# Moving large loads, norm pieces, weight means and modulation copies in a three-layer transformer kernel

## The chip, the cores and the metric

The kernel runs on one core of one Trainium2 chip. The metric is device time in microseconds of one execution; the lower, the better. The core has five engines that each work through their own instruction stream in order: TensorE (PE, with its weight loads shown as PEld), VectorE (DVE), ScalarE (ACT), GpSimd (POOL) and SyncE (SP). A DMA is an instruction in the stream of the engine that issues it; the data are then moved by 16 DMA engines.

## The reference

x is [4, 512, 288] in float32: B = 4 batches of T = 512 tokens with C = 288 features, and a condition vector of 288 for each batch. The computation is a rotation of the features and three transformer layers:

```
x = rotate(x)                                       # x + (z R - z) U^T, z = x U, U from a QR of P, R = expm(skew(silu(c) W^T + b))
layer 1, 2:
  shift_a, scale_a, gate_a, shift_m, scale_m, gate_m = split(silu(c) @ W_ada + b_ada, 6)
  h = layernorm(x) * (1 + scale_a) + shift_a
  q, k, v = split(h @ W_qkv + b_qkv)                # 16 heads of 18; layer 2 normalises q and k per head, with gains
  x = x + gate_a * (softmax(q k^T / sqrt(18)) v @ W_proj + b_proj)
  h = layernorm(x) * (1 + scale_m) + shift_m
  x = x + gate_m * (gelu(h @ W1 + b1) @ W2 + b2)    # hidden size 1152
layer 3: the same attention; its MLP is a mixture of 4 experts, each token through its best 2
```

## The kernel before

**Stages.** The rotation comes first (some 150 us of the profile), then twelve attention blocks n = 0 to 11 (three layers of four batches, n = 4·layer + batch) in the function `attend`, with the MLP of the block before after each block of layers 1 and 2, and at the end the experts over 19 tiles of 256 tokens. The attention blocks lie between about 160 and 1,600 us.

**One block.** `attend` runs 32 steps. A step issues one `maxima` (two matmuls into PSUM tile p_s, and a reduction on VectorE) for a group of heads ten steps ahead, and one `weigh` (two matmuls into p_st, and an exponential on ScalarE into a tile e). p_s and p_st take turns in the two buffers of the PSUM tag "big"; so each p_st waits until the exponential of the step before has read its buffer, and each p_s until the last reduction has. Every second step takes two e tiles into `sum_values` (p_av), and every eighth copies the sum (o) with ScalarE and sends it out with DMAs (sd, od).

**Work beside the steps.** The rest of a step is taken from two lists of generators. `fill` yields pieces of TensorE work with a cost: the projections of the next block (p_qk, p_var, p_v), the output projection of the last block (p_o), the transposes of normalised rows (p_t), and in n=0 the modulations of layers 2 and 3 (`modulations`, p_mod and p_modT). `norms` yields pieces of VectorE work, one for each step: four statistics, the reciprocal square root, and four scaled rows xn for each `normalize`. What is left of both is issued when the 32 steps are over, and `layernorm` issues what is left of its own norm before it transposes.

**Means of the weights.** Layer 2 normalises its heads; for that `center_heads(1)` takes the mean of each head's 18 columns off the weights: three reductions on VectorE (two pieces of wqk, and brow), each followed by a multiplication and an addition on POOL. It is called before n=2.

**Loads.** `load` issues on SP's queue, pinned to the program's order. Weights are loaded by it during the steps: `load_mlp` (6 DMAs, 2.9 MB) at step 17 and `load_attn` (14 DMAs, 1.5 MB) at step 24 of n=1 and n=5; `fill_table` copies the experts' weights from their tensors into one table in device memory (etab), half an expert at step 20 of each of n=2 to 9. SP also issues the small transfers that carry q, k, v, o and the softmax sums through scratch tensors (qd, store, sd, od, oc, rd, rb). Each DMA carries one of eight completion semaphores, in rotation over the whole program; before it is issued, its engine waits for the last DMA that had the same one, unless that is known to have landed.

**Order.** Most instructions stand as a scheduler places them from the order in which the generators issue them; loads and everything in the rotation are pinned.

The loop that hands out pieces, in short:

```
for step in range(8 * NG):
    for begin in loads.get(step, ()):
        begin()
    maxima(ahead, mstep); E.append(weigh(G, s))
    if s % 2 == 0: give_values()
    next(norms, None)
    while left > 0: cost = next(fill, "end") ...
```

Of the kernel before, what the change touches and what calls it, by code (L numbers as in the profile page):

```python
# [16 lines left out]
B, T, C = 4, 512, 288  # L17
NT = 4
KC, KP = 3, 96
# [4 lines left out]
NG = 4  # L24
# [23 lines left out]
def cond_seq_kernel(ctx: ExitStack, tc: tile.TileContext, a: dict, out: bass.AP):  # L48
    nc = tc.nc
# [17 lines left out]
    dma = nc.sync.dma_start  # L67
# [11 lines left out]
    def pmm(name):  # L79
        return ps.tile([128, 512], F32, tag="mm", name=name, bufs=3)  # L80
# [7 lines left out]
    def row(v):  # L88
        return v.rearrange("(o n) -> o n", o=1)
# [49 lines left out]

    WA, WM = [], []  # L140

    def load(t, src):
        tc.keep_in_program_order(dma(t, src))

    def load_features(t, src):

# [35 lines left out]
    def center_heads(l):  # L182

        wqk, brow = WA[l][0], WA[l][3]
        parts = wqk[:, 0:KW, :], wqk[0:STRIPS * TAIL, KW:, :]
        for i, t in enumerate([w.rearrange("p k (h d) -> p (k h) d", d=HD) for w in parts]
                              + [brow.rearrange("p (h d) -> p h d", d=HD)]):
            m = wattn.tile([t.shape[0], t.shape[1], 1], F32, tag=f"wmean{i}", name=f"wmean{i}", bufs=1)
            vector.tensor_reduce(m, t, AX.X, ALU.add)
            nc.gpsimd.tensor_scalar_mul(m, m, -1.0 / HD)  # L190
            nc.gpsimd.tensor_add(t, t, m.to_broadcast(list(t.shape)))

    def projection_bias(l):

        wqk, wv, wp, brow, bv = WA[l]
        p = pmm(f"p_bv{l}")
        for m in range(NO):
            r = slice(0, QP if m < NO - 1 else LO)
            matmul(p[0:64, :C], bv[r, m, :], wp[r, m, :], start=(m == 0), stop=(m == NO - 1))
        vector.tensor_add(wp[0:64, NO - 1, :], wp[0:64, NO - 1, :], p[0:64, :C])  # L200
# [82 lines left out]
    def load_ada(n):  # L283

        w, bias = (("L1_cond_W_ada", "L1_cond_b_ada"), ("L2_cond_w_ada", "L2_cond_b_ada"),
                   ("L3_cond_w_adaln", "L3_cond_b_adaln"))[n // 2]
        wa = was[n] = borrow(n % 2, f"wa{n}", KP + 1, 3 * KC * C).rearrange("p (k n) -> p k n", k=KC)
        cols = slice(n % 2 * 3 * C, (n % 2 + 1) * 3 * C)
        load(wa[0:KP], a[w][:, cols].rearrange("(k p) n -> p k n", p=KP))
        load(wa[KP:KP + 1, KC - 1, :], row(a[bias][cols]))  # L290
# [6 lines left out]
    def modulations(ns):  # L297

        for n in ns:
            l, half = divmod(n, 2)  # L300
            if half == 0:
                mt = mts[l] = const.tile([128, 4, KW + 1, B], F32, name=f"modT{l}")
                nc.gpsimd.memset(mt, 0.0)
            gr = mods.tile([B, C], F32, tag="gr", name=f"gr{n}")
            p = pmm(f"p_mod{n}")
            for k in range(KC):
                for s in range(3):
                    matmul(p[s * 32:s * 32 + B, :C], scT[0:kk(k), k, :],
                           was[n][0:kk(k), k, s * C:(s + 1) * C], start=(k == 0), stop=(k == KC - 1))
                yield 0.5  # L310
            for s in range(2):
                q = (2 * half + s) * 32
                scalar.copy(md[q:q + B], p[s * 32:s * 32 + B, :C])
            scalar.copy(gr, p[64:64 + B, :C])
            dma(gtab[n * B:(n + 1) * B], gr)
            if half and l < 2:
                br = mods.tile([B, C], F32, tag="br", name=f"br{l}")
                load(br, row(a[("L1_cond_b_fc2", "L2_cond_b2")[l]]).to_broadcast([B, C]))
                nc.gpsimd.tensor_mul(br, br, gr)
                dma(btab[l], br)  # L320
            if n == 5:
                sr = mods.tile([B, C], F32, tag="br", name="sr")
                scalar.activation(sr, p[32:32 + B, :C], AF.Copy, bias=1.0)
                dma(mrow.rearrange("s b c -> (s b) c")[0:B], md[64:64 + B])
                dma(mrow.rearrange("s b c -> (s b) c")[B:2 * B], sr)
                dma(mrow.rearrange("s b c -> (s b) c")[2 * B:], gr)
            if n + 2 < 6:
                load_ada(n + 2)
            if half:
                if l:  # L330
                    yield "later"
                pt = pmm(f"p_modT{l}")
                for k in range(KW + 1):
                    w = 128 if k < KW else TAIL
                    transpose(pt[:w, k * 128:(k + 1) * 128], md[:, k * 128:k * 128 + w], ident)
                    for i in range(1 if k < KW else STRIPS):
                        scalar.copy(mts[l][i * TAIL:i * TAIL + w, :, k, :],
                                    pt[:w, k * 128:(k + 1) * 128].rearrange("p (s r) -> p s r", r=32)[:, :, :B])
                for s in (1, 3):
                    nc.gpsimd.tensor_scalar_add(mts[l][:, s], mts[l][:, s], 1.0)  # L340
                modT.append(mts[l])
                yield 0.6
# [20 lines left out]
    with tc.tile_pool(name="l0", bufs=1) as l0, tc.tile_pool(name="l0w", bufs=2) as l0w, \  # L363
# [199 lines left out]
        main, fills, side = skew_and_exp(), clear(), itertools.chain(project_P(), first_modulations())  # L563
# [466 lines left out]
    with tc.tile_pool(name="attn", bufs=2) as at:  # L1030
# [99 lines left out]

        def maxima(G, step):

            n, g = divmod(G, NG)
            j, hp = divmod(step, 2)
            p = pbig(f"p_s{G}_{step}")
            for i in range(2):
                r = slice((2 * hp + i) * HS, (2 * hp + i + 1) * HS)
                matmul(p[:, i, :], Q[n % 2][r, g, j * 128:(j + 1) * 128], K[n % 2][r, g, :], start=True, stop=True)
            vector.tensor_reduce(M[G % 2][:, j, 2 * hp:2 * hp + 2, HD:HD + 1], p, AX.X, ALU.max)

        def take_maxima(G):

            n, g = divmod(G, NG)
            p = pmm(f"p_m{G}")
# [74 lines left out]
        def attend(n, fill, total, norms, loads):  # L1219


            left, strips = 0.0, False
            for step in range(8 * NG):
                g, s = divmod(step, 8)
                G = NG * n + g
                for begin in loads.get(step, ()):
                    begin()
                ahead, mstep = divmod(8 * G + s + LOOK, 8)
                if ahead < NG * NB:
                    while ahead // NG not in there:  # L1230
                        next(fill)
                    maxima(ahead, mstep)
                E.append(weigh(G, s))
                filled = strips
                if strips:
                    left -= next(fill)
                    strips = False
                if s == 8 - 2 and G + 1 < NG * NB:
                    take_maxima(G + 1)
                    left -= 0.6  # L1240
                left += total / (8 * NG) + (0.5 if s % 2 else -0.5 if ready else 0.0)
                if s % 2 == 0:
                    give_values()
                next(norms, None)
                while left > 0:
                    cost = next(fill, "end")
                    if cost == "end":
                        break
                    if cost == "strips":
                        if filled:  # L1250
                            strips = True
                            break
                        continue
                    if cost == "later":
                        if filled:
                            break
                        continue
                    filled = True
                    left -= cost or 0.0
                if s % 2:  # L1260
                    ready.append((G, s // 2))
            for _ in fill:
                pass
            for _ in norms:
                pass
# [49 lines left out]
        E, ready, PO, S, there, norms = [], [], [None], {}, set(), {}  # L1315
# [34 lines left out]
        for n in range(NB):  # L1350
            l, b = divmod(n, B)
            last = n and divmod(n - 1, B)

            fill, side, total = [], [], 0.0
            loads = {}
            if n == 1 or n == B + 1:
# [2 lines left out]
                loads[24] = [lambda l=l, names=names: WA.append(load_attn(l + 1, *names))]  # L1359
                names = (("L1_cond_W_fc1", "L1_cond_b_fc1", "L1_cond_W_fc2"), ("L2_cond_w1", "L2_cond_b1", "L2_cond_w2"))[l]  # L1360
                loads[17] = [lambda l=l, names=names: WM.append(load_mlp(l, *names))]
            if n == 2 or n == B + 2:
                if l == 0:
                    center_heads(1)
            if n + 1 < NB:
                if n:
                    new = project(n + 1, norm)
# [11 lines left out]
            if n and last[0] < 2:  # L1379
                norm2 = normalize(last[0], 1, last[1], n - 1)  # L1380
                side.append(norm2)
                fill.append(layernorm(last[0], 1, last[1], hT[1], norm2))
                total += 1.8
            if n == NB - 3:
                prepare_routes()
                load_mods(0)
                load_mods(1)
# [204 lines left out]
```

## Time and profile before

| | us |
|---|---|
| median of 3 runs | 2043.26 |
| lowest and highest | 2023.45, 2050.5 |
| profiled execution | 2027.39 |
| its span, first to last instruction | 2025.7 |

The mean granted TensorE clock of the profiled execution was 0.963. ScalarE's largest group is the 384 exponentials, at 1023 ns each, VectorE's the 384 reductions, at 1226 ns:

```
L60 ACT ACTIVATE e<-p_st 128x1024 f32<-128x1024 f32 x384 | 392.7, 1023 | 643.2 <-PE p_st L60 639.7
L60 DVE TENSOR_REDUCE store<-p_s 128x2 f32<-128x1024 f32 x384 | 470.5, 1226 | 363.0 <-PE p_st L60 348.3
```

A row names the line, the engine, the operation, what is written from what, the shapes and the count; then the busy time and the mean of one in ns; then the idle time of the engine just before and what ended most of it. L60 is the line of a recording helper, through which most instructions pass, so groups are told apart by their tiles. In a waits view, a row gives the waiting engine and its tile, what it waited for, the total in us, the number of waits and the longest. In a timeline, the columns are start and length in us, engine, line, operation and tiles, the count, and in brackets the idle time before and what ended it. A "q" after an engine's name (SPq) is its queue, which issues DMAs and waits.

The work of `load` on SP in the profiled execution: `load_mlp` was issued at 349.25 and 878.80 us, `load_attn` at 66.72, 357.78 and 894.35 us.

### The profile page before, as it was taken

How to read it: one execution, taken by the hardware profiler on the slowest of the kernel's cores; microseconds unless marked ns; L12 is line 12 of the kernel's file. 1: busy time of each engine (PE TensorE's matmuls, PEld its weight loads, DVE VectorE, ACT ScalarE, POOL GpSimd, SP SyncE). 2: the span in 40 equal slices, each digit the busy share in tenths (PEclk: the TensorE clock that was granted, in tenths of full speed). 3: DMA queues.
4: the chain of work that ended last, by engine and by line, in shares of the span. 5: the costliest groups of instructions: out<-in, count | busy, mean ns of one | idle time of the engine just before them, and what ended most of it. 6: DMA issues, size and time to landing. Idle time of an engine off the chain costs nothing. (4 is left out here: it accounts for less than half of the span.)

```text
span 2025.7 us, 26353 instructions
## 1 busy us (share of the span) xinstructions
PE 1864.3 (92%) x10269; PEld 925.1 (46%) x10269; DVE 928.4 (46%) x1953; ACT 782.7 (39%) x1169; POOL 252.3 (12%) x362
## 2 busy tenths in 40 slices
PE   6769989999999999989999999999998899999997
PEld 4554222343523434435234343343332267788886
DVE  6764646446165263552652625535566534211111
ACT  5122355434354354443543444434444433122121
POOL 1000000010011010110110000010010132323232
PEclk9578999999999999999999999999999999999999
DMA  3311123312212123151110502144222265576673
GB/s 99 73 41 53 44 62 110 90 35 93 44 53 70 26 78 52 41 140 49 53 41 20 112 18 72 57 93 97 76 56 64 89 233 187 177 239 210 208 248 98
DMA packets 90283, 187.23 MB, mean 92 GB/s; under 512 B 26317, under 2 KB 51320, under 8 KB 87666
## 3 DMA queue, kind: packets, MB, share of 16 engines
q1 hardware_dynamic: 78326, 103.39, 19.3%
q0 software_dynamic: 11248, 79.79, 12.1%
q10 hardware_dynamic: 584, 2.36, 0.4%
q8 instruction: 81, 1.33, 0.3%
q14 instruction: 44, 0.36, 0.1%
HBM read 152.49 MB, written 55.45 MB: 103 GB/s over the span
## 5 line engine op out<-in xcount | busy, mean ns | idle before, releaser
L60 ACT ACTIVATE e<-p_st 128x1024 f32<-128x1024 f32 x384 | 392.7, 1023 | 643.2 <-PE p_st L60 639.7
L60 DVE TENSOR_REDUCE store<-p_s 128x2 f32<-128x1024 f32 x384 | 470.5, 1226 | 363.0 <-PE p_st L60 348.3
L60 PE MATMUL p_s<-store 32*128 32x512 f32 x1536 | 443.9, 651 | 75.4 <-DVE store L60 69.1
L60 PE MATMUL p_st<-store 32*128 32x512 f32 x1536 | 442.0, 651 | 1.3 <-DVE store L60 1.3
L60 PEld LDWEIGHTS p_s<-store 32*128 32x128 f32 x1536 | 117.9, 185 | 324.8 <-DVE store L60 253.2
L60 PE MATMUL p_av<-e,store 128*32 128x512 f32 x1536 | 211.2, 623 | 1.1 <-ACT e L60 1.1
L60 PE MATMUL p_he<-hTe,store 128*128 128x256 f32 (+1 forms) x1026 | 185.4, 387 | 1.4 <-DVE hTe L60 1.4
L60 PE MATMUL p_ye<-store,hide 128*128 128x288 f32 x684 | 171.1, 409 | 0.1
L697 POOL TENSOR_TENSOR x<-x,gated 128x288 f32<-128x288 f32 x80 | 63.9, 799 | 814.1 <-DVE gated L60 814.1
L60 PEld LDWEIGHTS p_he<-hTe,store 128*128 128x128 f32 (+1 forms) x1026 | 149.5, 189 | 33.7 <-issue 13.2
L60 PE MATMUL p_qk<-hT,wqk 128*126 128x512 f32 (+1 forms) x360 | 164.2, 621 | 0.3 <-DVE store L60 0.3
L60 ACT ACTIVATE hide<-p_he,store 128x256 f32<-128x256 f32 x171 | 68.2, 479 | 234.7 <-PE p_he L60 189.5
L60 PE MATMUL p_h<-hT,w 128*128 128x512 f32 (+1 forms) x432 | 153.5, 610 | 4.6 <-DVE store L60 4.6
L60 PEld LDWEIGHTS p_ye<-store,hide 128*128 128x128 f32 x684 | 128.4, 190 | 37.1 <-ACT hide L60 2.5
L60 DVE TENSOR_TENSOR gated<-p_y,gate 128x288 f32<-128x288 f32 x32 | 14.6, 458 | 282.6 <-PE p_y L60 282.6
L60 PE MATMUL p_y<-w,hid 128*128 128x288 f32 x576 | 141.8, 407 | 0.0
L60 PEld LDWEIGHTS p_y<-w,hid 128*128 128x128 f32 x576 | 108.8, 190 | 35.5 <-issue 6.1
L60 PEld LDWEIGHTS p_st<-store 32*128 32x128 f32 x1536 | 118.1, 186 | 9.0 <-issue 6.7
L60 PEld LDWEIGHTS p_h<-hT,w 128*128 128x128 f32 (+1 forms) x432 | 62.1, 189 | 91.2 <-issue 84.9
L60 PE MATMUL p_o<-wp,oc 126*128 126x288 f32 (+1 forms) x288 | 91.7, 438 | 0.8 <-DVE oc L60 0.8
L60 PEld LDWEIGHTS p_qk<-hT,wqk 128*126 128x126 f32 (+1 forms) x360 | 47.7, 178 | 95.2 <-issue 88.9
L1541 POOL DMA_INDIRECT out_dram<-ye,idx x38 | 60.9, 1603 | 209.9 <-issue 111.7
(248 smaller groups left out, 1672.4 us busy)
## 6 DMA issues: line engine op xcount, KB each, us to landing
store<-qd SPq DMA_DIRECT2D x192, 72.0 KB
qd<-stage SPq DMA_DIRECT2D x48, 252.0 KB
od<-o SPq DMA_DIRECT2D x192, 36.0 KB
rd<-rd SPq DMA_DIRECT2D x12, 576.0 KB
oc<-od SPq DMA_DIRECT2D x24, 252.0 KB
rb<-rd SPq DMA_DIRECT2D x24, 252.0 KB
etab<-in_L_cond_w_dram SPq DMA_DIRECT2D x4, 1296.0 KB
etab<-in_L_cond_w_dram SPq DMA_DIRECT2D x8, 576.0 KB
```

Source lines behind the costliest of these rows:

```text
L60: ins = f(*args, **kw)
L697: nc.gpsimd.tensor_add(x[b][:, j, :], x[b][:, j, :], t)
L1541: tc.keep_in_program_order(nc.gpsimd.indirect_dma_start(out_rows if t >= EARLY else out_rows[0:2 * T], bass.IndirectOffsetOnAxis(ap=idx[:, ...
```

## The change

Four edits. Loads that `attend` starts at a given step are issued on ScalarE's queue; other loads stay on SP's. From step 20 on, `norms` gives two pieces a step. `center_heads` becomes a generator with one of the three means as a piece, in the list of norms of n=2. And `modulations` yields after the copies that follow its last products and no longer between the products and the copies; the mark "later", with which `attend` put off p_modT of layers 2 and 3 until the next step, goes.

```diff
+    queue = [nc.sync]
+
     def load(t, src):
-        tc.keep_in_program_order(dma(t, src))
+        tc.keep_in_program_order(queue[0].dma_start(t, src))
...
     def center_heads(l):
...
             vector.tensor_reduce(m, t, AX.X, ALU.add)
             nc.gpsimd.tensor_scalar_mul(m, m, -1.0 / HD)
             nc.gpsimd.tensor_add(t, t, m.to_broadcast(list(t.shape)))
+            yield True
...
     def modulations(ns):
...
                 for s in range(3):
                     matmul(p[s * 32:s * 32 + B, :C], scT[0:kk(k), k, :],
                            was[n][0:kk(k), k, s * C:(s + 1) * C], start=(k == 0), stop=(k == KC - 1))
-                yield 0.5
+                if k < KC - 1:
+                    yield 0.5
             for s in range(2):
                 q = (2 * half + s) * 32
                 scalar.copy(md[q:q + B], p[s * 32:s * 32 + B, :C])
...
             if n + 2 < 6:
                 load_ada(n + 2)
+            yield 0.5
             if half:
-                if l:
-                    yield "later"
                 pt = pmm(f"p_modT{l}")
...
         def attend(n, fill, total, norms, loads):
...
             for step in range(8 * NG):
                 g, s = divmod(step, 8)
                 G = NG * n + g
+
+                queue[0] = nc.scalar
                 for begin in loads.get(step, ()):
                     begin()
+                queue[0] = nc.sync
...
-                    if cost == "later":
-                        if filled:
-                            break
-                        continue
                     filled = True
                     left -= cost or 0.0
+                if step >= 5 * NG:
+                    next(norms, None)
                 if s % 2:
                     ready.append((G, s // 2))
...
-            if n == 2 or n == B + 2:
-                if l == 0:
-                    center_heads(1)
...
+            if n == 2:
+                side.append(center_heads(1))
```

## The prediction

> **What bounds the kernel now.** I read four views, in this order: the page's first two parts, the waits of TensorE, the timelines around TensorE's longest gaps, and the queue views of SP and ScalarE. The page and the waits:
>
> ```profile
> span 2025.7 us, 26353 instructions
> PE 1864.3 (92%) x10269; PEld 925.1 (46%) x10269; DVE 928.4 (46%) x1953; ACT 782.7 (39%) x1169; POOL 252.3 (12%) x362
> PE p_s L60 <- DVE store L60: 69.1, 130, 2.2
> PE p_t L60 <- DVE xn L60: 6.3, 4, 1.6
> PE p_s L60 <- issue: 4.0, 1, 4.0
> PE p_modT L60 <- ACT md L60: 2.5, 2, 2.0
> ```
>
> TensorE is busy 92%, and in its 161 us of idle no DMA is named as releaser. What delays TensorE costs time nearly one to one; what delays SP costs nothing until a tile is missed. ScalarE's 39% looks roomy, but one step of `attend` is a tight ring: p_st goes out, ScalarE makes e from it, and the next p_st needs that PSUM buffer back, because the two `big` buffers alternate between p_s and p_st. In the timeline:
>
> ```profile
> 346.51 0.59 ACT L60 COPY o<-p_av 128x512 f32<-128x512 f32 x1
> 347.61 1.02 ACT L60 ACTIVATE e<-p_st 128x1024 f32<-128x1024 f32 x1 [0.51 <-PE p_st L60]
> 349.31 0.70 PE L60 MATMUL p_st<-store 32*128 32x512 f32 x2
> ```
>
> The exponential ends at 348.63 and the next p_st starts at 349.31: 0.68 us to spare. Elsewhere the spare is 2 to 3 us, counted from the start of ScalarE's instruction before it, since the queue can go on while that one runs.
>
> Gaps of TensorE, with what they do to the clock:
>
> ```profile
> 290.46 0.47 PE L60 MATMUL p_modT<-ident,md 128*128 128x128 f32 x1 [1.99 <-ACT md L60]
> 428.92 0.70 PE L60 MATMUL p_s<-store 32*128 32x512 f32 x2 [2.22 <-DVE store L60]
> 644.35 1.50 PE L60 MATMUL p_t<-ident,xn 128*128 128x128 f32 x4 [1.58 <-DVE xn L60]
> 893.53 1.19 PE L60 MATMUL p_s<-store 32*128 32x512 f32 x1 [4.05 <-issue]
> ...
> 644.00:648.00 4.00, 3.63 (x16) 1.87 (x16) 1.32 (x4) 1.55 (x2) 0.00 (x0) 0.64 0.00 0
> 894.00:898.00 4.00, 4.00 (x18) 0.95 (x14) 2.36 (x4) 1.02 (x1) 0.00 (x0) 0.54 0.78 209
> ```
>
> The last two are rows of the windows view (stretch, busy time of each engine, then granted clock, DMA share, GB/s). In the 4 us around the 1.58 us gap the clock was 0.64, about 3 us at half speed, with a little more in the next window: some 1.7 us lost besides the gap. After the 4.05 us gap it was 0.54 for 4 us: 1.8, and half a microsecond before it. After the 1.99 us gap the same sequence, from one p_s over p_m and p_av to the next p_s, took 4.69 us (292.56 to 297.25) where it took 2.65 at full speed (268.41 to 271.06): 2.0 lost.
>
> **The change part by part.**
>
> *Large loads.* The build moves 76 DMAs from SP to ScalarE, in twelve groups: 6 of `load_mlp` and 14 of `load_attn` in n=1 and n=5, and `fill_table`'s eight groups (6 or 3 DMAs) at step 20 of n=2 to 9. In ScalarE's order each group stands whole ahead of the next exponential, which queues behind it; behind that wait p_st, everything later on TensorE, and VectorE's reductions. Each issue takes its queue's time, and it first waits until the earlier DMA on its completion semaphore has landed (eight semaphores go round). On SP:
>
> ```profile
> 349.25 2.01 SPq L143 DMA_DIRECT2D w<-in_L_cond_W_fc_dram  x4
> 351.77 1.07 SPq L143 DMA_DIRECT2D w<-in_L_cond_W_fc_dram  x1
> 894.35 1.82 SPq L143 DMA_DIRECT2D wqk<-in_L_cond_w_qkv_dram  x4
> 901.18 0.23 SPq L143 DMA_DIRECT2D brow<-in_L_cond_b_qkv_dram  x1
> 903.15 0.25 SPq L143 DMA_DIRECT2D wp<-in_L_cond_b_proj_dram  x1
> 478.41 3.90 SPq L143 DMA_DIRECT2D etab<-in_L_cond_w_dram  x6
> 784.59 0.67 SPq L143 DMA_DIRECT2D etab<-in_L_cond_w_dram  x1
> 785.31 3.90 SPq L143 DMA_DIRECT2D etab<-in_L_cond_b_dram  x2
> ```
>
> brow waited until 901.18 for the first wqk piece, issued by 894.74: such a piece needs about 6.3 us to land. Now group by group, time of the block less ScalarE's spare:
> - `load_mlp`, n=1: the third DMA waits for the first, 1.2 MB, to land. A piece of half the size needed 6.3 us; a later DMA on this one's semaphore was issued at 357.02, so at most 7.3. I take 7.0: block from 346.5 to 356.5, exponential 8.9 late, less 0.7: 8.2.
> - `load_mlp`, n=5: it waits for the four od transfers of the o just copied, and then for a piece of its own weights; about 881.7 where the exponential stood at 874.3: 7.4 less 0.9: 6.5.
> - `load_attn`: 894.35 to 903.40 on SP is 9.05 (8.9 in the first one, from 66.72), less 3.1: 5.9, twice 11.8.
> - `fill_table` first half: 3.9 less 3.1 is 0.8 in n=2 and 8. In n=4 and 6 the last DMA comes round to a semaphore of its own group, so 1.2 of issue, 6.3 of landing and 0.6 make 8.1, less a spare of 2.1: 6.0 each. Together 13.6. Bounds for the latter two: 1.8 (landed at once) and 8 (a table-to-table copy twice as slow).
> - second half: 4.6 to 4.7, less 2.1 in n=3 and 5, less 3.1 in n=7 and 9: 8.4 together.
>
> Sum 48.5 (8.2 + 6.5 + 11.8 + 13.6 + 8.4). Clock: six stalls of 5 us and more at the 2.3 of the 4.05 us gap, and half of four stalls of 1.6 to 2.6 at 1.7: 17. Against it, VectorE catches up during a stall, and the p_s wait that would have come next (0.3 to 1.3 us) falls away: 12 times 0.7, 8. Net 57.5 lost.
>
> A rule is to be weighed here. The Trainium skill ("DMA: Bandwidth & Descriptors", Issuing engines are not separate DMA queues) says that starting DMAs on several engines saves only the sequencer's time for starting them, usually small beside the DMA itself. SP agrees that the saving is worthless: it waited 280.6 us for o copies alone. But "usually small" would put 76 issues at next to nothing on ScalarE too, and the sum would end at the gains below; the rows show 0.23 to 3.1 us an issue, and waits besides. I take the rows.
>
> What SP gains: its small transfers no longer stand behind large ones. No TensorE wait names them, so 0, except the 4.05 us gap at 893.53, in which TensorE waited for nothing shown while DMA was full; with its half clock 6.5. The same bytes move in the same steps, so it can as well recur: I take half, 3.2, bounds 0 and 6.5, or a second such gap, −6.5.
>
> *Two VectorE pieces in late steps.* `next(norms)` is called twice from step 20. By the build, the four xn of the MLP's norm, which in n=3 to 6 stood together behind the last reduction (1.44 us for four), now come one and two reductions earlier; the p_t gap of 1.58 falls away four times, with its clock: 4 x 3.3 = 13.1. Each late step carries up to 0.6 us more on VectorE; where the ring is tight p_s waits: 1 back. Gain 12, bounds 5 and 14. On the clock the skill's rule ("TensorE: Matmul & The Clock Gate", Part 1: The HAM clock gate) says that half rate follows an idle window of about 3.4 us; by it the 1.58 us gaps would cost no clock and this gain would be 6. The windows row of 0.64 decides for 12.
>
> *Means one by one.* Three reductions (2.00 us for two and 0.73, on VectorE in one go at 425.08, before n=2's first p_s reduction) go one to a step; POOL's part follows each, and POOL is idle 88%. The gap of 2.22 and its 1.7 go; the largest piece, 1.3 us, about fills VectorE's idle between two reductions (1.23 to 1.5 in the timeline), 0.3 back: gain 3.6. The weights are next read in n=3.
>
> *p_mod's copies.* They are issued in the step of the last products, and without "later" p_modT of layer 1 follows them directly, two steps sooner; layer 2's comes two exponentials after its copies. So layer 2's gap goes, 1.99 and 2.0 of clock, less 0.4 as its transposes now wait for an exponential as layer 1's did (1.00 against 0.56). But layer 1 gets the same gap: e, 1.02, and two md copies, 0.80, end about 1.6 us after p_mod does; 1.6 and 1.0 of clock (it cools in some such gaps), less 0.4. Gain 1.4, bounds −1 and 4. gtab and br leave SP and POOL earlier; nobody waits. In the rotation at the start the copies move by half a step under VectorE's chain: 0.
>
> Gains 3.2 + 12 + 3.6 + 1.4 = 20.2; 57.5 − 20.2 = +37. The profiled execution took 2027.4 us (its span 2025.7), so 2064 for one like it; it stood 16 below the median of the three runs, and on that median, 2043.3, it is 2080.
>
> **The rivals.**
> (1) ScalarE's blocks are short: not slower. Place: the twelve groups. If a load lands sooner on a queue of its own and the issues overlap the exponential before them, a block shrinks to its issue time, and the spare covers it. For: a spare of 2 to 3 us in ten of the twelve. Against: the third DMA of n=1 cannot be issued before 1.2 MB have landed. It decides where the stalls with their clock come under 20 us in all, 1.7 a group; with 3 left it is 2043 − 17 = 2026.
> (2) The round of semaphores ties the two queues together: ScalarE waits for SP transfers that are themselves held up, and SP's stores come due on the semaphores of ScalarE's w1 and w2. For: a store issue that took 3.63 us at 352.88, behind w2 on the same queue. Against: SP mostly waits for ScalarE, so it has caught up by then. Blocks 3 us longer in all twelve groups: 2080 + 36 = 2116.
> (3) The loads hinder nobody, before or after, and the gaps on VectorE's side come back elsewhere: 2043.
>
> **How the numbers follow.** Chances: forecast 0.57, its own range 2055 to 2105; (1) 0.2; (2) 0.19; (3) 0.04. A measurement of this kernel tells about 2% (41 us) from no change. Over 2% slower: 0.42 of the forecast, as 37 lies close under 41, and (2): 0.43. Over 2% faster needs every gain, no stall and 20 us more: 0.03. Within: 0.54. The range, 2026 to 2113, goes from (1)'s figure to just under (2)'s; half of each and little of the forecast are left out, 2 in 10.
>
> **What would show it.** DMA rows of `load` on ScalarE, 4 to 10 us a group; behind each an idle of TensorE before p_st or the next p_s, over 40 us in all, with clock windows of 0.5 to 0.7 after it; no p_t gap in n=3 to 6, and none over 1 us at n=2's first p_s; a p_modT gap that moves from layer 2 to layer 1. It is wrong if these stalls stay under 20 us in total, if ScalarE's groups last under 3 us, or if the p_t gaps stay.

## The result, and the profile after

| | before | changed |
|---|---|---|
| median, us | 2045.36 | 2105.94 |
| lowest and highest | 2023.45, 2050.50 | 2101.37, 2113.02 |
| runs | 4 | 4 |
| profiled execution, us | 2027.39 | 2103.59 |
| its mean granted TensorE clock | 0.963 | 0.936 |

The changed kernel is slower: the ratio is 1.032, with a 95% interval of 1.0239 to 1.0402. The forecast was 2080, in a range that went to 2113. The two profiled executions differ by more than the medians, by 76 us. Some 16 of it is a stretch of half clock in block 11, which the profiled execution of before happens not to have. By their times most runs of before have it too: they lie in two clusters, about 2027 and 2047 us, called the lower and the upper one below, and the last section tells of it. All four runs of the changed kernel have clocks of 0.935 to 0.938, like its profiled one, which has the stretch; three of the four of before are in the upper cluster. So the 60.6 us between the medians is like against like.

The first lines of the changed kernel's page, and rows of its view of TensorE's waits (tile, releaser, total in us, number, longest):

```profile
span 2101.9 us, 26331 instructions
PE 1924.6 (92%) x10269; PEld 945.3 (45%) x10269; DVE 929.4 (44%) x1953; ACT 783.0 (37%) x1169; POOL 252.5 (12%) x362
...
PE p_s L60 <- DVE store L60: 73.4, 138, 1.8
PE p_st L60 <- DVE store L60: 12.7, 8, 2.4
PE p_st L60 <- ACT e L60: 10.4, 5, 6.4
PE p_av L60 <- ACT e L60: 3.5, 2, 2.4
PE p_modT L60 <- ACT md L60: 1.4, 1, 1.4
```

The reader should see two things. First, new waits: p_st now waits for ScalarE's exponential (10.4 us) and for VectorE behind it (12.7, where it was 1.3 before), and p_av for e (3.5, where it was 1.1); the p_t wait is gone from the list and one of two p_modT waits is left. Second, these waits are far less than the time lost. TensorE's busy time rose by 60 us with the same 10,269 matmuls: more of them ran at half clock (the mean clock fell from 0.963 to 0.936).

How the one becomes the other is seen best at the smallest group of loads, `fill_table`'s in block 8. ScalarE's timeline, then TensorE's, then two rows of the windows view (the block from its first to its last exponential, and the 11 us after the group; the columns are the stretch, the busy time of PE, PEld, DVE, ACT and POOL, the granted clock, DMA share and GB/s):

```profile
1322.35 1.02 ACT L60 ACTIVATE e<-p_st 128x1024 f32<-128x1024 f32 x1 [1.37 <-PE p_st L60]
1322.36 3.74 ACTq L145 DMA_DIRECT2D etab<-in_L_cond_w_dram  x6
1326.20 1.02 ACT L60 ACTIVATE e<-p_st 128x1024 f32<-128x1024 f32 x1 [2.83 <-DMA etab<-in_L_cond_w_dram]
```

```profile
1322.19 1.92 PE L60 MATMUL p_o<-wp,oc 126*128 126x288 f32 x6
...
1328.94 1.75 PE L60 MATMUL p_st<-store 32*128 32x512 f32 x4 [1.33 <-DVE store L60]
1330.62 3.55 PE L60 MATMUL p_o<-wp,oc 126*128 126x288 f32 x6
```

```profile
1269.50:1360.60 91.10, 85.45 (x484) 29.00 (x483) 53.48 (x78) 42.30 (x52) 3.40 (x5) 0.94 0.23 71
1329.00:1340.00 11.00, 11.00 (x38) 3.87 (x38) 3.48 (x9) 2.44 (x4) 0.79 (x1) 0.53 0.08 26
```

Six issues hold ScalarE for 3.74 us. The exponential behind them comes 2.83 us late, and of that 1.33 reach TensorE. But the clock then falls to half for 10.2 us in which TensorE is busy all the time: the same six p_o matmuls take 3.55 us, where they took 1.92 just before. The block lasts 91.1 us, and 84.6 where the loads are on SP (below): here a stop of 1.33 us went with 6.5 lost. The last section shows the same stop without a fall of the clock.

The largest stop is in block 5, where `load_mlp`'s group waits for transfers to land. (Which one ends a wait is read from the trace's semaphore records: the second DMA was issued at 902.76, after a small copy of SP's had landed at 902.74, and the third at 906.87, after another at 906.85.)

```profile
899.06 1.01 ACT L60 ACTIVATE e<-p_st 128x1024 f32<-128x1024 f32 x1
899.90 0.40 ACTq L145 DMA_DIRECT2D w<-in_L_cond_w_dram  x1
899.96 0.58 ACT L60 COPY o<-p_av 128x512 f32<-128x512 f32 x1
902.76 4.91 ACTq L145 DMA_DIRECT2D w<-in_L_cond_w_dram  x3
907.72 0.44 ACTq L145 DMA_DIRECT2D b<-in_L_cond_b_dram  x1
908.19 1.46 ACTq L145 DMA_DIRECT2D w<-in_L_cond_w_dram  x1
909.70 1.02 ACT L60 ACTIVATE e<-p_st 128x1024 f32<-128x1024 f32 x1 [9.16 <-DMA w<-in_L_cond_w_dram]
```

```profile
910.78 2.08 PE L60 MATMUL p_st<-store 32*128 32x512 f32 x4 [6.41 <-ACT e L60]
```

From the first issue to the last ScalarE does nothing but one copy for 9.7 us; TensorE stands 6.41 us.

### The profile page after: what moved, and what is told of

It is laid out like the page before. It is cut to its first block, busy times and chain, and to the rows that moved or that the text cites. A ratio compares the mean times of both kernels' runs of the same rounds, so it can differ in the third digit from the quotient of the medians.

```text
span 2101.9 us, 26331 instructions
## 1 busy us (share of the span) xinstructions
PE 1924.6 (92%) x10269; PEld 945.3 (45%) x10269; DVE 929.4 (44%) x1953; ACT 783.0 (37%) x1169; POOL 252.5 (12%) x362
## 3 DMA queue, kind: packets, MB, share of 16 engines
q8 instruction: 81, 1.33, 0.3%
## 5 line engine op out<-in xcount | busy, mean ns | idle before, releaser
L60 PE MATMUL p_st<-store 32*128 32x512 f32 x1536 | 458.2, 673 | 23.1 <-DVE store L60 12.7
L60 PE MATMUL p_av<-e,store 128*32 128x512 f32 x1536 | 219.3, 645 | 3.5 <-ACT e L60 3.5
L60 PEld LDWEIGHTS p_y<-w,hid 128*128 128x128 f32 x576 | 108.8, 190 | 35.5 <-issue 6.1
L60 PE MATMUL p_o<-wp,oc 126*128 126x288 f32 (+1 forms) x288 | 109.3, 506 | 0.8 <-DVE oc L60 0.8
L60 PEld LDWEIGHTS p_h<-hT,w 128*128 128x128 f32 (+1 forms) x432 | 62.0, 189 | 91.2 <-issue 84.9
L60 PEld LDWEIGHTS p_av<-e,store 128*32 128x32 f32 x1536 | 31.0, 111 | 127.8 <-issue 121.1
```

The lines of the kernel that those rows point to most:

```text
L60: ins = f(*args, **kw)
```

## The experiments

The theory: the loads in groups on ScalarE cost the time, because a group stands whole ahead of the exponentials; the three other edits gain less than the prediction gave them. Rivals: a wait that the four edits make together; the second VectorE piece as the culprit; and a loss of each issue's time on ScalarE wherever it stands.

A table of block lengths carries most of what follows (us from the first to the last exponential of a block, from each profile's timeline; "start" is the first exponential of block 0):

| kernel | start | 0 | 1 | 2 | 3 | 4 | 5 | 6 | 7 | 8 | 9 | 10 | 11 |
|---|---|---|---|---|---|---|---|---|---|---|---|---|---|
| before | 215 | 83.4 | 84.9 | 87.4 | 92.7 | 92.7 | 99.7 | 92.7 | 83.8 | 83.9 | 84.9 | 96.5 | 86.4 |
| changed | 217 | 83.1 | 97.7 | 91.1 | 96.5 | 97.5 | 113.3 | 97.4 | 86.1 | 91.1 | 86.4 | 96.5 | 102.9 |
| loads on SP | 218 | 86.3 | 85.6 | 84.5 | 91.9 | 92.1 | 98.4 | 91.9 | 84.5 | 84.6 | 84.9 | 96.9 | 101.6 |
| loads alone | 215 | 83.5 | 97.6 | 91.3 | 98.6 | 98.3 | 116.3 | 99.7 | 85.5 | 91.1 | 86.5 | 98.0 | 101.6 |
| tables alone on ScalarE | 217 | 83.6 | 85.6 | 86.9 | 93.9 | 99.4 | 109.6 | 97.4 | 86.0 | 89.5 | 86.4 | 98.0 | 86.5 |
| one a step, ScalarE | 218 | 83.4 | 85.6 | 84.5 | 91.9 | 93.5 | 105.0 | 91.8 | 84.6 | 84.6 | 84.9 | 96.9 | 86.5 |
| groups on POOL | 216 | 82.0 | 85.6 | 84.7 | 103.2 | 92.6 | 108.5 | 91.9 | 84.5 | 84.6 | 84.9 | 98.5 | 99.9 |
| pieces early in a group | 219 | 83.4 | 84.8 | 83.8 | 91.0 | 91.0 | 98.4 | 91.0 | 83.8 | 83.9 | 84.9 | 96.5 | 103.2 |
| the same, p_mod as before | 215 | 83.4 | 84.9 | 83.8 | 91.0 | 90.9 | 98.2 | 90.9 | 83.8 | 83.9 | 84.9 | 96.5 | 86.4 |
| and one a step on SP | 216 | 82.7 | 84.9 | 84.0 | 91.0 | 90.9 | 90.9 | 90.9 | 83.8 | 83.9 | 84.9 | 100.3 | 86.4 |
| changed, no late pieces | 218 | 83.1 | 97.2 | 91.0 | 93.8 | 98.7 | 118.1 | 95.3 | 85.4 | 91.1 | 86.4 | 96.5 | 103.3 |
| loads on SP, dense matmul | 218 | 83.6 | 85.6 | 84.5 | 91.9 | 92.2 | 98.4 | 91.8 | 84.5 | 84.6 | 84.8 | 96.8 | 90.0 |
| one a step on SP, dense matmul | 215 | 82.7 | 84.9 | 84.0 | 91.0 | 90.9 | 90.9 | 91.0 | 83.8 | 83.9 | 84.8 | 100.3 | 102.6 |

What lies between the blocks differs by some 2 us at most; what follows block 11 takes 406 to 413 us. The medians of before that the ratios below refer to are 2044.89 us (13 runs) for the first four experiments, 2046.04 (31 runs) for the next four and 2046.80 (16 runs) for the last three. A median can lie in either cluster, so where a kernel's runs fall in both, the text also compares cluster with cluster.

**The changed kernel with its loads back on SP.**

```diff
-                queue[0] = nc.scalar
+                queue[0] = nc.sync
                 for begin in loads.get(step, ()):
                     begin()
```

> The changed kernel with its loads back on SP; the other three edits stay. Theory (ScalarE's stream is held up by the loads, everything else gains a little): below the kernel before by 10 to 25 us, about 2028, no wait of p_st for an exponential over 1 us, blocks n=3 to 6 each about 3 us shorter than before. Rival (the VectorE pieces or the modulation copies cost time too, for instance in n=11, which grew by 16 us): still above the kernel before, 2060 or more, with n=11 as long as in the changed kernel (103 us).

Measured: 2046.91 us, ratio to before 1.0009 (0.9969 to 1.0049). The loss is gone with the queue, and the gain of the other three edits isn't there: cluster against cluster, in their means, this version stands 3 to 5 us above before. Rows of its waits, in the same columns:

```profile
PE p_s L60 <- DVE store L60: 79.3, 146, 1.7
PE p_s L60 <- issue: 3.8, 1, 3.8
PE p_modT L60 <- ACT md L60: 1.4, 1, 1.4
PE p_st L60 <- DVE store L60: 1.3, 1, 1.3
```

The p_t wait of 6.3 us of before is gone as predicted, but the p_s wait is 79.3 where it was 69.1: 10.2 more. And the gap of about 4 us in block 5 is there as before, which on ScalarE it was not.

**The kernel before with the loads alone moved.**

```diff
+                queue[0] = nc.scalar
                 for begin in loads.get(step, ()):
                     begin()
+                queue[0] = nc.sync
```

> The kernel before with the loads on ScalarE alone. Theory: slower than the changed kernel by what the other edits gain, 10 to 20 us: 2115 to 2125. Rival (the other edits cost time): faster than the changed kernel, 2060 to 2095.

Measured: 2101.73 us, ratio 1.0262 (1.0183 to 1.0341), 56.8 us over before. Its four runs lie at 2085 and 2095 (clock 0.95) and at 2109 and 2111 (0.94); cluster against cluster they stand 62 to 64 us above before, and in the profiles blocks 1 to 9 are 62 us longer. The loads alone are the loss, and the other three edits together give back little.

**The changed kernel without the second VectorE piece.**

```diff
-                if step >= 5 * NG:
-                    next(norms, None)
```

> The changed kernel without the second VectorE piece in late steps. Theory: the gap before p_t comes back in n=3 to 6, 12 us slower than the changed kernel, about 2117. Rival (the late pieces brought the 51 us stretch at half clock in n=11): n=11 back at 87 us, 2090 to 2095.

Measured: 2104.08 us, ratio 1.0277 (1.0213 to 1.0341), 2 us from the changed kernel. Neither the 12 us of the theory nor the rival shows: block 11 takes 103.3 us here too. In blocks 3 to 6 two values are lower and two higher than in the changed kernel, so nothing can be told of the second piece beside the loads.

**Only the tables' copies on ScalarE, weights on SP.**

```diff
-                queue[0] = nc.scalar
+                queue[0] = nc.scalar if step == 20 else nc.sync
```

> Of the moved loads only the expert table's eight groups stay on ScalarE; the layers' weights are back on SP. Theory: the eight groups hold ScalarE for 4 to 7 us each with 2 to 3 us to spare, so about 25 to 30 us above the kernel with all loads on SP, and the four weight groups make up the rest, 27 us with their clock. Rival (only the waits for a landing cost, not the issues): 5 to 10 us above it.

Measured: 2078.04 us, ratio 1.0184 (1.0122 to 1.0245), 31 us over the version with all loads on SP; in the profiles blocks 1 to 9 are 36.5 us longer. The eight table groups can make over half of the loss. How much of it is theirs in the changed kernel this doesn't settle, since 11.2 us of it lie in block 5, where the group's DMAs waited for weights on the other queue: the second was issued at 897.25 us, 3.45 us after the first, when a piece of the weights on SP with the same completion semaphore had landed (897.23). In the changed kernel the same group had no such wait.

**On ScalarE, but one DMA a step.** `load` puts its DMAs into a list, from which each step takes one:

```diff
+                for _ in range(-(-len(later) // (8 * NG - step))):
+                    tc.keep_in_program_order(nc.scalar.dma_start(*later.pop(0)))
```

> The changed kernel, its loads still on ScalarE's queue, but no longer in groups: of what a step releases, one DMA is issued in each step (two when fewer steps are left in the block than DMAs). In the changed kernel's trace the 76 issues take 48.6 us of ScalarE's stream, 0.3 to 0.8 us each (the last of the four second halves 3.0 to 3.2 us), and the twelve groups hold it for 3.8 to 9.8 us at a stretch. Theory (a group longer than ScalarE's spare and than the steps in flight stops TensorE and lets its clock fall; issues one by one fit into the spare): the loss goes down to the four 3 us issues and a little more, 2046 to 2065 us, near the version with the loads on SP (2046.9), and the half-clock stretches in blocks 1 to 9 go. Rival (ScalarE has no spare; each issue is lost wherever it stands): about 48 us of loss stay, 2085 to 2105 us.

Measured: 2049.72 us, ratio 1.0060 (1.0016 to 1.0105), 56 us under the changed kernel (its upper cluster 50 under, and 7 over that of the version on SP). Blocks 1 to 3 and 6 to 9 are within 0.2 us of the version on SP, so ScalarE does have room for the issues; it has none for a group. Block 5 is the exception, at 105.0. There, on ScalarE and on TensorE:

```profile
901.39 2.24 ACTq L1240 DMA_DIRECT2D wqk<-in_L_cond_w_qkv_dram  x1
903.68 1.02 ACT L60 ACTIVATE e<-p_st 128x1024 f32<-128x1024 f32 x1 [1.75 <-PE p_st L60]
913.92 1.81 ACTq L1240 DMA_DIRECT2D wqk<-in_L_cond_w_qkv_dram  x2
915.83 1.02 ACT L60 ACTIVATE e<-p_st 128x1024 f32<-128x1024 f32 x1 [11.12 <-DMA wqk<-in_L_cond_w_qkv_dram]
```

```profile
916.90 2.08 PE L60 MATMUL p_st<-store 32*128 32x512 f32 x4 [7.47 <-ACT e L60]
```

One single DMA was not issued until 913.92 and kept the next exponential back by 11.12 us. By the trace's semaphore records it waited for a row of the table, issued on the same queue at 897.68 with the same completion semaphore, to land at 913.89. Two copies of o on SP waited likewise for table copies that ScalarE had issued (issued at 910.69 and 913.70, after landings at 910.68 and 913.69). So it isn't the number of issues alone: one DMA that has to wait stops the engine whose stream it is in.

**The groups on POOL's queue.**

```diff
-                queue[0] = nc.scalar
+                queue[0] = nc.gpsimd
```

> The changed kernel with the same grouped loads on POOL's queue in place of ScalarE's (POOL is busy for about an eighth of the span). Theory (what costs is the stop of ScalarE, whose exponentials every step waits for, not the leaving of SP's queue): no loss against the version with the loads on SP (2046.9), and the 3.8 us gap of TensorE in block 5 that stands there is gone, which with its clock is 4 to 6 us: 2038 to 2047 us. Rival (POOL's additions and multiplications of the normalization and of the residual stand behind the groups as the exponentials do on ScalarE): the blocks 1 to 9 grow as they do on ScalarE, over 2070 us.

Measured: 2062.05 us, ratio 1.0086 (1.0036 to 1.0137). The theory fell in two blocks, 3 and 5, which are 11 and 10 us longer than with SP; most others are as there. TensorE's new waits, of 7.41 us in block 3 and 11.55 in block 5, are for copies of the queries:

```profile
PE p_s L60 <- DMA store<-qd: 19.0, 2, 11.6
631.46 1.22 PE L60 MATMUL p_s<-store 32*128 32x512 f32 x1 [7.41 <-DMA store<-qd]
```

The rival has POOL's own work stand behind the group. POOL's timeline in block 3, then the same additions with the loads on SP:

```profile
610.21 1.56 POOL L1081 TENSOR_SCALAR stage<-stage,qn_b 126x512 f32<-126x512 f32 x1 [3.62 <-DVE stage L60]
611.72 1.10 POOL L145 DMA_DIRECT2D etab<-in_L_cond_w_dram  x1
612.82 1.54 POOL L145 DMA_DIRECT2D etab<-in_L_cond_b_dram  x2
618.73 1.56 POOL L1081 TENSOR_SCALAR stage<-stage,qn_b 72x512 f32<-72x512 f32 x1 [4.37 <-issue]
```

```profile
614.67 1.57 POOL L1081 TENSOR_SCALAR stage<-stage,qn_b 126x512 f32<-126x512 f32 x1 [3.61 <-DVE stage L60]
623.18 1.56 POOL L1081 TENSOR_SCALAR stage<-stage,qn_b 72x512 f32<-72x512 f32 x1 [6.95 <-issue]
```

The second addition starts 8.52 us after the first with the group between them and 8.51 without it, so here the group did not hold POOL up. What grew is the copies' own time. The one for which TensorE waited set out on SP at 614.28 and landed at 631.42, 17.1 us later; with the loads on SP the same copy took 2.0 us (618.78 to 620.74). While it was under way, 1.48 MB of the group moved (613.8 to 632.9 us). With the loads on SP no table transfers fall there: SP issued this group at 517.28, at the end of block 2. So neither the theory nor the rival names the cause in block 3; that the group's transfers slowed the copies fits these times, but no run isolates it.

**The second piece only in the first four steps of a group of heads** (loads on SP).

```diff
-                if step >= 5 * NG:
+                if step >= 5 * NG and s < 4:
                     next(norms, None)
```

> The three smaller edits with the loads on SP (2046.9 us), the second VectorE piece of the late steps only where the step is one of the first four of its group of eight. With the pieces in all twelve late steps the 1.6 us gap of TensorE before the normalization's transposes goes in blocks 3 to 6, but the waits of the row maxima's matmuls for VectorE grow there from 3.8 to 6.2-6.5 us. Theory (the second pieces stand ahead of the maxima on VectorE, and so turn the one wait into the other): with fewer of them the maxima's waits come back towards 3.8-5 us while the gap stays away, blocks 3 to 6 shrink by 1 to 2.5 us each: 2037 to 2043 us. Rival (four pieces are too few, or the maxima's waits have another cause): blocks 3 to 6 between 91.5 and 93 us, as before and as now, 2045 to 2049 us.

Measured: 2024.51 us, ratio 0.9937 (0.9890 to 0.9984); its runs lie in two clusters, 2019 to 2028 and 2039 to 2043, as those of before do (2024 to 2030, 2044 to 2053). Cluster against cluster, in their means, it is 5 to 7 us faster. To see why, the waits of TensorE inside block 3: of before, then with the second piece in all late steps (loads on SP), then with this version:

```profile
PE p_s L60 <- DVE store L60: 3.8, 6, 1.5
PE p_t L60 <- DVE xn L60: 1.6, 1, 1.6
```

```profile
PE p_s L60 <- DVE store L60: 6.1, 10, 1.5
```

```profile
PE p_s L60 <- DVE store L60: 4.3, 7, 1.5
PE p_t L60 <- DVE xn L60: 1.1, 1, 1.1
```

The second piece took the p_t wait away (1.6) and put 2.3 on p_s, since it stands on VectorE ahead of a reduction. With fewer pieces only 0.5 of the p_t wait goes and only 0.5 comes on p_s, and the half clock after it stays away all the same: 92.7, 91.9 and 91.0 us for the block. In blocks 1, 2, 7 and 8, where there was no p_t wait to win, the full version costs 0.7 us each.

**A dense matmul where the last block waits** (loads on SP, all late pieces).

```diff
         def weigh(G, step):
             p = pbig(f"p_st{G}_{step}")
+            if n == NB - 1 and step == 0:
+                matmul(p[:, 0, :], ident, K[n % 2][:, g, :], start=True, stop=True)
```

> The three smaller edits with the loads on SP (2046.9 us), and in the last block one more dense matmul (128x128 by 512 columns, overwritten by the products that follow) at the first step of each group of heads, where TensorE waits 1.3 us for VectorE. In five of six profiles the last block has a stretch of 44 to 51 us in which TensorE runs at half its clock though it is busy all the time; the block takes 102 us with it and 86 us without, and the runs of the kernel before lie in two clusters, about 2024-2033 and 2043-2050 us. Theory (the stretch begins where TensorE has done little in the microseconds before): the dense work keeps the clock up, the last block takes 86 to 89 us, 2030 to 2034 us in most runs. Rival (the stretch has a cause outside this block, or comes by chance): the last block still 102 us in most runs, 2046 to 2050 us.

Measured: 2040.46 us, ratio 1.0003 (0.9964 to 1.0043), block 11 at 90.0 us in its profile, runs from 2031 to 2046. Its runs are spread over that range and don't fall into two clusters. Inconclusive by itself; the last run below says more.

**The modulations' copies as before** (means and early pieces kept, loads on SP).

```diff
-                if k < KC - 1:
-                    yield 0.5
+                yield 0.5
...
-            yield 0.5
             if half:
+                if l:
+                    yield "later"
```

> The kernel before with the means among the steps' pieces and the second VectorE piece in the first four steps of the last groups; the modulations' copies as before, the loads on SP as before. The profiles with the copies moved have their first exponential at 216 to 219 us, those without at 215: in the phase that computes the first weights, the copies stand ahead of an activation for which TensorE's next products wait. Theory (the moved copies cost there and give nothing later): first exponential back at 215 us, and against the same kernel with the moved copies (2024.5, its lower runs 2019-2028 and its upper 2039-2043) 2 to 4 us less: lower runs 2017 to 2024. Rival (the start differs by chance, and the moved copies save 1.4 us later): no change or 1 to 2 us more.

Measured: 2037.80 us median of 10, ratio 0.9939 (0.9904 to 0.9975); six of its runs are in the upper cluster, so the median stands above that of the version with the moved copies, but cluster by cluster it is lower: 2017 to 2022 against 2019 to 2028, and 2037 to 2041 against 2039 to 2043, in the means 3.5 and 2.6 us. The first exponential is back at 215. Where the moved copies cost, in the rotation at the start (ScalarE and TensorE of the version that has them):

```profile
106.40 0.79 ACT L60 COPY md<-p_mod 4x288 f32<-4x288 f32 x2 [0.92 <-PE p_mod L60]
107.20 0.39 ACT L60 COPY gr<-p_mod 4x288 f32<-4x288 f32 x1
107.62 0.37 ACT L60 COPY sq<-p_sq 128x256 f32<-128x256 f32 x1
107.89 0.16 ACT L60 ACTIVATE Nm<-g_bc 64x1 f32<-64x1 f32 x1
```

```profile
108.04 0.65 PE L60 MATMUL p_sq<-sq,two 64*64 64x256 f32 x4 [1.25 <-ACT Nm L60]
```

The three copies, 1.2 us, and the wait for p_mod in front of them stand ahead of Nm, an activation in a chain from VectorE over ScalarE to TensorE that nothing else covers. Without the move Nm (at 106.72 there) comes before them.

**And the loads one a step on SP.** As in the run on ScalarE, `load` puts its DMAs into a list; in short:

```diff
                 for begin in loads.get(step, ()):
                     begin()
+                for _ in range(-(-len(later) // (8 * NG - step))):
+                    tc.keep_in_program_order(dma(*later.pop(0)))
```

> The kernel of the run without the moved copies, and the large loads on SP's queue one DMA a step (two when fewer steps are left) in place of groups. In block 5 of the kernels with grouped loads on SP TensorE waits 3.8 to 4.5 us right after the weight load of the feed-forward network was issued, while a copy of the projected queries waits its turn behind it on SP's queue. Theory (the group holds up that copy): the gap and the half-clock stretch after it go, block 5 shrinks from 98.4 to 91-93 us, the median falls by 5 to 7 us. Rival (the copy waits for the transfers themselves and not for the issues ahead of it): block 5 stays at 98 us, no change.

Measured: 2018.93 us (2013.67 to 2034.27, 7 runs), ratio 0.9890 (0.9853 to 0.9926): the fastest of all. Four of its runs are in the lower cluster and the median with them, while 15 of the 16 of before are in the upper one; cluster against cluster, in their means, it is 11 to 14 us under before, about 0.6%, and 3 to 6 us under the same kernel with the groups. Block 5 in the windows view, with the group on SP and with one DMA a step:

```profile
817.00:915.20 98.20, 87.67 (x494) 29.50 (x494) 59.95 (x88) 48.09 (x62) 11.18 (x10) 0.97 0.33 94
```

```profile
817.60:908.50 90.90, 84.61 (x494) 28.63 (x494) 59.94 (x88) 48.19 (x61) 11.27 (x10) 1.00 0.43 104
```

The same 494 matmuls, 7.3 us less, at full clock: the 4 us gap goes with the group. With the group ahead of it the copy of the queries set out 5.3 us after its tile was written (876.09 against 870.82) and took 8.5 us to land; with one DMA a step it was 1.4 and 6.0 us. So the issues ahead of the copy are the larger part and the transfers beside it the rest; spreading the loads changes both, and no run parts them. Block 10 lost 3.8 us, with 13.7 us at half clock in place of 6.8; the cause is open.

**The same with the dense matmul.**

> The kernel with the spread loads on SP and with the dense matmul at the first step of each group of heads in the last block. Theory (the half-clock stretch of the last block is rarer or shorter with it): upper runs come down towards the lower ones, median 2016 to 2024 us, last block 86 to 92 us. Rival (the dense matmul has no hold on the stretch): two clusters about 16 us apart as without it, last block 102 us in the upper one.

Measured: 2033.44 us, 4 runs from 2032.73 to 2038.87, ratio 0.9946 (0.9927 to 0.9965), block 11 at 102.6. All its runs are in the upper cluster: the dense matmul does not keep the half clock away. In its profile block 11 has it in two stretches, 13.7 and 23.9 us, in place of one.

## Why the prediction came out as it did

The direction and the cause were right. That the number came out in the range is in part luck: the stops were put too high and the clock too low, and these two errors nearly cancel. The forecast of +37 fell short of +60.6 because two of the gains were not there and the tables' groups cost more than was put down for them.

**The loads: a cost of the right order, from the wrong parts.** Predicted 57.5, before SP's relief. In blocks 1 to 9 of the profiles the changed kernel stands 58.7 us over the version with the loads on SP, but that version has SP's gap in block 5, which cost 7.3; without it the loads cost about 66. The prediction made its sum of 48.5 us of stops and 17 of clock. The new waits behind the groups come to 24 us over the kernel. Other waits fell away, so in these blocks TensorE has only 15.3 us more idle (72.6 against 57.3), or about 19 with SP's gap taken out of the comparison: half of what was put down, and close to the 20 us under which the prediction called itself wrong. The other 43 us are busy time: 81.8 us ran at half clock, against 6.8, and half of these 75 us is 37. So the clock is the larger part. A late exponential doesn't stop TensorE by its own length, since TensorE first works off what stands before it; the 2.83 us of block 8 came out as 1.33. And the clock was then at half for 6.8 to 13.7 us in six of these blocks, for 27.3 in block 5 and not at all in two, where the prediction had counted 2.3 us of loss, or 4.6 at half, at most for a stop. So the weights' groups came out near the sum (blocks 1 and 5, with the one table group in the latter: by the prediction's terms 35.5, measured 27.0, or 34 without SP's gap in the comparison) and the tables' groups were put too low (the other seven blocks: 21.5 predicted, 31.7 measured; blocks 2 and 8 nearly nothing predicted, 6.6 and 6.5 measured). Of `load_mlp` in block 5 the prediction had 6.5, and TensorE stood 6.41.

**The late pieces: 12 predicted, nearly nothing measured.** This is the step that failed most, and in it the term of what comes back. The p_t gaps went in all four blocks, and the half clock after them, as predicted. But "where the ring is tight p_s waits: 1 back" was wrong: with the loads on SP the p_s waits rose by 10.2 us over the kernel. Block by block against before, with the means' gain in block 2 taken from the version with early pieces, the second pieces gain 3.5 us in blocks 3 to 6 and lose 3.2 in blocks 1, 2, 7, 8 and 10. The twelve steps were costed for the four blocks that have a gap, and not for those that have none.

**The means: right.** Predicted 3.6; block 2 fell from 87.4 to 83.8 in the version with the early pieces, and the 2.2 us gap before its first p_s is gone. No run moved the means alone; but blocks 1, 7 and 8 are as before in that version, so its other edits cost and give nothing there, and the 3.6 can be put down to the means.

**p_mod's copies: 1.4 gain predicted, 2.6 to 3.5 lost.** The gap moved from layer 2 to layer 1 as predicted (one p_modT wait of 1.4 in place of two), but 6.8 us of half clock went with it, and block 0 takes 83.4 us with the copies moved and without: nothing gained. And the last clause failed: "in the rotation at the start the copies move by half a step under VectorE's chain: 0". They moved ahead of ScalarE's own link of that chain.

**SP's relief: 3.2 predicted.** The gap of block 5 went when the groups left SP for ScalarE, and a longer one came in its place. That it comes of the group is shown by the run with one DMA a step on SP, where the same bytes, spread over the steps, leave no gap and block 5 is 7.3 us shorter; half of 6.5 was too careful. The wait for "nothing shown" was for a copy of the queries: it landed at 893.44 us and TensorE went on at 893.53. Nor do "the same bytes move in the same steps": SP issued the tables' groups of blocks 3 to 6 before those blocks began (block 3's at 513.67 us in the profile of before), ScalarE within them (at 635.59).

With these sizes the sum is 66, less 7.3 (SP's relief), less 0.3 (pieces), less 3.6 (means), plus 3 (copies), or about +58, beside +60.6 between the medians of four runs each.

The two rules that were weighed: the saving by several issuing engines is indeed not worth anything, but that an issue is usually small beside its DMA (the Trainium skill, "DMA: Bandwidth & Descriptors", Issuing engines are not separate DMA queues) doesn't make it small for the engine that issues it. Here 76 issues took 48.6 us of ScalarE's stream, and in the blocks where they came one a step without waiting they cost 0.2 us at most. And a half clock only after an idle window of about 3.4 us (the same, "TensorE: Matmul & The Clock Gate", Part 1: The HAM clock gate) would have put blocks 2 and 8 at about 1.3 us each; the rows show 10.2 us of half clock after 1.33 us of idle. A rule that every such stop brings the half clock would be as wrong (last section).

Of the rivals, (1), that the groups fit into the spare, and (3) fell with the loads alone at +56.8. Of (2), that the round of semaphores ties the two queues together, the mechanism shows in block 5: there `load_mlp`'s group waited for two small copies of SP's, 2.5 and 3.8 us, and with one DMA a step SP's copies of o waited for ScalarE's table copies. It did not lengthen all twelve groups: those of the tables last 3.7 to 6.8 us, none longer than predicted.

## What to carry to other kernels

A DMA is an instruction in the stream of the engine that starts it, and takes its issue time there and its wait; so start large loads one at a time between the steps, on an engine whose next instruction nobody waits for, and never in a group ahead of a link of the inner loop. An engine's idle share (61% on ScalarE) says nothing about this: what counts is the spare before the one instruction that stands behind the group. Moving the group to an engine that is idle most of the time isn't enough either: on POOL the small copies beside it took 17 us in place of 2. When a piece is moved into earlier steps to end one wait, count it in every block that has these steps, not only in those that have the wait.

## What the runs showed that was not expected

**A short stop can cost by the clock, and need not.** In block 8 of the changed kernel 1.33 us of TensorE's idle were followed by 10.2 us at half clock with TensorE busy throughout. With the tables alone on ScalarE, block 2 has the same group and the same stop:

```profile
488.47 1.13 PE L60 MATMUL p_st<-store 32*128 32x512 f32 x4 [1.33 <-DVE store L60]
489.53 1.92 PE L60 MATMUL p_o<-wp,oc 126*128 126x288 f32 x6
```

Here p_o takes 1.92 us, the granted clock of the 11 us after the stop is 1.00, and the block is 2.4 us longer than on SP, where it was 6.6 in the changed kernel. The length of the one stop doesn't decide it, and what does stays open. So the cost of a table group can differ with the same stop.

**A long stretch of half clock in a full TensorE.** In seven of the thirteen profiles block 11 takes 100 to 103 us, in six of these with one stretch of 44 to 51 us at half clock; in five it takes 86 and in one 90, with nearly the same instructions. (The expectation above that speaks of five of the first six miscounts: it was four.) The version with the loads on SP, then before, in the windows view over the same kind of work:

```profile
1600.00:1640.00 40.00, 38.88 (x100) 12.28 (x98) 6.67 (x21) 9.83 (x13) 6.28 (x7) 0.51 0.29 108
```

```profile
1600.00:1620.00 20.00, 18.88 (x88) 6.61 (x84) 4.40 (x12) 9.00 (x12) 6.13 (x7) 1.00 0.58 217
```

TensorE is 97% busy in the one and 94% in the other. The block takes about 102 us with the stretch and 86 without; runs of before lie at 2023 to 2030 or at 2043 to 2054 us, none between. It comes with kernels with the change and without, and so explains nothing of it, but a comparison of a few runs, or of one profile with another, can be off by 16 us through it. What brings it on stays open: one dense matmul in the gaps ahead did not keep it away.
